# Masking the first key block with a product on VectorE instead of a matmul on TensorE

## The chip, the cores and the metric

The kernel runs on one core of one Trainium2 chip. The metric is the device time of one execution in microseconds (us). The engines are TensorE (PE in the profile; its weight loads are listed apart as PEld), VectorE (DVE), ScalarE (ACT), GpSimd (POOL) and SyncE (SP), which issues most DMAs.

## The reference, cut to what matters

For 32 sequences of 256 tokens with 256 features, a conditioned state-space block is computed first, and its output goes through two layers of windowed attention and feed-forward:

```python
x = x + ffn(cond(x, cond_2048, ...), ...)

# cond: a projection, a causal convolution of 4 taps, a layer norm, then a scan over the tokens
h = clip(h * ad + bd * xt, -10, 10);  yt = ct @ h          # 16 states x 512 channels

# ffn: two layers of
q, k, v = split(shift_token(x) @ wqkv)                     # 8 heads of 64
q, k = rotary(l2norm(q) * qs), rotary(l2norm(k) * ksc)
sim = 8 * q @ k.T                                          # windows of 128 tokens
mask = (i < j) | (i > j + WINDOW) | (j == -1)              # own window and the one before it
x = x + softmax(where(mask, -max, sim)) @ v @ wo
x = x + (a * gelu(g)) @ w2 + b2                            # feed-forward after a layer norm
```

A sequence has two windows of 128 tokens. The first block of keys (keys 0 to 127) is read by all 256 queries: for queries 0 to 127 only keys at or before the query count, for queries 128 to 255 only keys at most 128 tokens back. The second block of keys is read by queries 128 to 255 alone.

## The kernel before

**Groups and units.** The 32 sequences form four groups of 8 (`GB`). Each group first goes through the state-space scan (`group_scan`), 256 steps in 8 chunks of 32, and then through two layers of attention and feed-forward, one sequence at a time. One sequence in one layer is called a unit here; there are 64 units, 16 for each group. The scan of group 0 runs alone at the start; the scans of groups 1, 2 and 3 run beside the units of the group before. In the last group no scan is left.

**Order.** The program writes an order out by hand: a unit has 8 stages (`ST`), and `stage(n, i, what)` puts a piece of work of unit n into stage i. After each stage `scan_to` lets the scan go on by its share of steps. Most of a unit's work overlaps with that of its neighbours: in a stage there may be the projections of the next unit, the scores of this one, and the feed-forward of the two or three before it. Each engine works through its own queue in the order that results, and `keep_in_program_order` pins some instructions there.

**PSUM.** All matmul results go through one pool of 8 banks (`ps_w`), whatever their use. A bank is free again when the engine that reads it is done, so TensorE can have to wait for a reader on another engine before it starts on unrelated work.

**Scores.** The attention computes scores transposed: keys on partitions, queries along the row. Two heads share 128 rows of the transposed queries and keys (64 features each), index r. In stage 2 `scores` works on two parts, and on one more in stage 3; a part is (kw, i0, n), a key block, a first pair of heads and a number of pairs. Key block 0 comes as two parts of two pairs, (0, 0, 2) and (0, 2, 2), and each fills two banks of 2 x 256 columns; key block 1 is one part of four pairs. In the first three groups (`apart` is false) the mask of key block 0 is written into the bank before the scores: a matmul of a bf16 identity with the mask tile `mask_t` (0 or -32768), L1200, and the products are added on top (L1227). These products are cut into four tiles of the array, 64 rows x 64 columns, since a half of 64 keys needs only 192 of the 256 queries. In the last group (`apart` is true) there is no mask matmul; the products run on two row tiles of 64 x 128 over all 256 queries.

**Exponentials and masks.** `exponentials` (L1239, ScalarE) turns the banks into `pT` tiles in SBUF. `mask` then zeroes what is left to mask: for key block 1 by GpSimd's affine select (L1250), and, in the last group, for key block 0 by VectorE's product with `mask_1`, a bf16 tile of zeros and ones (L1255), 128x512 an instruction and four of them a unit, in stages 3 and 4:

```python
masked = nc.vector.tensor_mul(p, p, bc(mask_1[:, 0:nq], 1, n))
```

**Afterwards.** Stage 7 forms the sums (L1264) and the values (L1282) from `pT`. In the next unit the sums make a round trip through DRAM, VectorE divides (L1322), and `project_out` (L1047) multiplies by wo.

**Names of the other lines.** L991: projection of q, k and v. L1007, L1012, L1017 on VectorE and L1015, L1021 on GpSimd: rotary embedding and norms. L1027: scaling by the norm, VectorE. L1036: transposes of q and k. L1402, L1413, L1420: the feed-forward's first product, its gelu on ScalarE, the product of the halves on VectorE. L1429, L1440: its second product and, on VectorE, the residual sum (`narrow`, in stages 3 and 4, ahead of the masks). L1448: the final sum on GpSimd, in the second layer only. Of the scan: L473 to L511 the convolution, shared by GpSimd (L480) and VectorE (L491, L511); L708 scaling a row on ScalarE; L718 a step on VectorE; L730 its read-out on TensorE; L781 and L801 sums and gates of the read-out on VectorE, each freeing a PSUM bank; L787 the transposes between them.

Of the kernel before, what the change touches and what calls it, by code (L numbers as in the profile page):

```python
# [19 lines left out]
P = 128  # L20
S = 256
# [17 lines left out]
W = 128  # L39
# [4 lines left out]
LN_EPS = 1e-5  # L44
CLIP = 10.0
MASKED = -1e30
MASKED_LOW = -32768.0


SCALES2 = 25.0  # L50
# [2 lines left out]
def bc(ap, axis, n):  # L53

    ap = ap.unsqueeze(axis)
    shape = list(ap.shape)
    shape[axis] = n
    return ap.broadcast_to(shape)
# [15 lines left out]
def kernel(  # L74
# [29 lines left out]
    nc = tc.nc  # L104
    B = xT.shape[2]
    L = wqkv.shape[1]
    NG = B // GB

    const = ctx.enter_context(tc.tile_pool(name="const", bufs=1))
# [35 lines left out]
    ident = const.tile([P, P], FP, tag="ident", name="ident")  # L145
# [17 lines left out]
    for j in range(NJ):  # L163
# [12 lines left out]

    mask_t = const.tile([P, 2 * W], BF, tag="mask_t", name="mask_t")
    ident_b = const.tile([P, P], BF, tag="ident_b", name="ident_b")  # L180
    nc.vector.tensor_copy(ident_b, ident)
    nc.gpsimd.memset(mask_t, 0.0)
    nc.gpsimd.affine_select(
        out=mask_t[:, 0:W], in_=mask_t[:, 0:W], compare_op=ALU.is_ge, fill=MASKED_LOW,
        base=0, pattern=[[1, W]], channel_multiplier=-1,
    )
    nc.gpsimd.affine_select(
        out=mask_t[:, W : 2 * W], in_=mask_t[:, W : 2 * W], compare_op=ALU.is_ge,
        fill=MASKED_LOW, base=0, pattern=[[-1, W]], channel_multiplier=1,
    )  # L190

    mask_1 = const.tile([P, 2 * W], BF, tag="mask_1", name="mask_1")
    nc.gpsimd.tensor_scalar(mask_1, mask_t, -1.0, None, ALU.is_ge)

    head_cols = const.tile([P, 2, 32], FP, tag="head_cols", name="head_cols")
    nc.gpsimd.memset(head_cols, 0.0)
# [27 lines left out]
    def program(ctx, exact):  # L224
# [9 lines left out]
        ps_w = ctx.enter_context(tc.tile_pool(name="psw", bufs=8, space=PSUM, reuse_waits="tile"))  # L234
# [822 lines left out]
        if exact:  # L1057
# [104 lines left out]
        class Attention:  # L1162
# [2 lines left out]

            def __init__(self, g, l):
                self.l = l

                self.apart = g == NG - 1
                self.qkv, self.rot, self.p, self.ps, self.o = {}, {}, {}, {}, {}  # L1170

            def project(self, b, w, a):
# [20 lines left out]

            def open_banks(self, kw, n):
                nq = S - kw * W
                banks = []
                for r in range(2):
                    sc = ps_w.tile([P, n, nq], FP, tag="w", name="sc")
                    if kw == 0 and not self.apart:
                        nc.tensor.matmul(  # L1200
                            sc, ident_b, bc(mask_t[:, 0:nq], 1, n), start=True, stop=False
                        )
                    banks.append(sc)
                return banks

            def scores(self, b, *parts):

# [5 lines left out]

            def products(self, b, kw, i0, n, banks):
                qT, kT, _ = self.qkv[b]
                nq = S - kw * W
                masked = kw == 0 and not self.apart
                nm = 2 if masked else 1
                mk = W // nm
                for i in range(n):  # L1220
                    for r in range(2):
                        rows = slice(r * DH, (r + 1) * DH)
                        for m in range(nm):

                            k0 = m * mk
                            q0, q1 = (k0, k0 + W + mk) if masked else (0, nq)
                            nc.tensor.matmul(  # L1227
                                banks[r][k0 : k0 + mk, i, q0:q1],
                                kT[rows, i0 + i, kw * W + k0 : kw * W + k0 + mk],
                                qT[rows, i0 + i, kw * W + q0 : kw * W + q1],  # L1230
                                start=not masked,
                                stop=not masked or i == n - 1,
                            )

            def exponentials(self, b, kw, i0, n, banks):
                nq = S - kw * W
# [245 lines left out]
        def stage(n, i, what, *args):  # L1482
            stages.setdefault(ST * n + i, []).append(partial(what, *args))

        def attend(n, at, b, nxt):

            stage(n, 0, at.turn, b, 1)
            stage(n, 2, at.scores, b, (0, 0, 2), (1, 0, HEADS // 2))
            stage(n, 3, at.scores, b, (0, 2, 2))
            stage(n, 3, at.mask, 1, 0)  # L1490
            if at.apart:
                for i, what in ((3, (0, 0)), (4, (0, 2))):
                    stage(n, i, at.mask, *what)
            stage(n, 7, at.sums, b)
            stage(n, 7, at.values, b)
            stage(n + 1, 0, at.put_sums)
            stage(n + 1, 1, at.load_sums)
            stage(n + 1, 2, at.invert)
            stage(n + 1, 2, at.put_inverse)
            stage(n + 1, 3, at.load_inverse)  # L1500
            stage(n + 1, 5, at.divide, b)
            stage(n + 1, 6, at.finish, b)
            if nxt is not None:
                for w in range(NW):
                    for i, a in ((0, 2), (1, 0), (1, 1)):
# [60 lines left out]
        for t in range(max(stages) + 1):  # L1566
# [3 lines left out]
            g, r = divmod(t + 1 + group - reload, group)  # L1570
# [124 lines left out]
```

## Time and profile before

| | us |
|---|---|
| median of 3 runs | 3545.71 |
| lowest, highest | 3545.69, 3548.17 |
| the profiled execution's own time | 3553.66 |
| its span, first to last instruction | 3551.9 |

| line | what | count | busy us | mean ns of one |
|---|---|---|---|---|
| L1200 | PE, mask product, 128x512 bf16 | 192 | 57.5 | 380 |
| L1227 | PE, products on four tiles, 192 columns | 1536 | 84.6 | 335 |
| L1227 | PE, products on two row tiles, 256 columns | 256 | 36.3 | 402 |
| L1239 | ACT, exponentials | 384 | 202.1 | 603 |
| L1255 | DVE, mask product, 128x512 | 64 | 49.7 | 817 |
| L718 | DVE, scan step | 1024 | 931.9 | 910 |

One execution is profiled, and its times are those of that execution. A float32 matmul that isn't a transpose shows as two records. Matmuls overlap in the array, so the mean length of one is longer than the time from one start to the next; where the cost of a block on TensorE matters, read the time from its first start to the start of what follows. In the order of time, "[0.74 <-DVE zT L801]" says that the engine was idle for 0.74 us before the instruction, and what ended the wait.

### The profile page before, as it was taken

What the parts mean: (1) busy time and instruction counts of PE and PEld (TensorE: products, weight loads), DVE (VectorE), ACT (ScalarE), POOL (GpSimd) and SP (SyncE); (2) the same over time, 40 slices, a digit from 0 to 9 for tenths busy, and PEclk for the clock granted to TensorE, in tenths of its full rate; (3) what the DMA queues carried; (4) which work ended last, traced back from release to release, by engine and by line L of the source; (5) the groups of instructions that cost most, each with busy time, mean ns of one, the idle gap of its engine ahead of it and who ended that gap; (6) DMA issues with size and microseconds to landing.
All of it is one profiled execution on the core that took longest, in us unless ns stands there. A gap on an engine that the chain in (4) does not pass through costs nothing.

```text
span 3551.9 us, 57690 instructions
## 1 busy us (share of the span) xinstructions
PE 3441.7 (97%) x20220; PEld 2263.7 (64%) x20220; DVE 2605.5 (73%) x5049; ACT 2037.4 (57%) x3663; POOL 1620.7 (46%) x1587
## 2 busy tenths in 40 slices
PE   7999989999999999999999999999999999999999
PEld 5445335666666666666666666666666777777777
DVE  4888898877878777877787778787777545555563
ACT  3666656656666656666566656666666444444442
POOL 4433455544545445544454556454443333333441
PEclk8999999999999999999999999999999999999999
DMA  6788765534454555544454445544444212011111
GB/s 183 211 219 217 200 174 153 135 113 134 125 143 138 150 144 150 139 121 126 123 144 131 139 147 146 145 115 129 124 138 118 63 37 62 13 31 35 37 28 38
DMA packets 487199, 436.72 MB, mean 123 GB/s; under 512 B 247155, under 2 KB 326516, under 8 KB 486772
## 3 DMA queue, kind: packets, MB, share of 16 engines
q1 hardware_dynamic: 402450, 420.94, 42.0%
q10 hardware_dynamic: 84450, 12.01, 2.1%
q8 instruction: 162, 2.65, 0.3%
q14 instruction: 137, 1.12, 0.1%
HBM read 384.06 MB, written 47.19 MB: 121 GB/s over the span
## 4 chain that ended last, share of the span: by engine, by line
PE 64%; DVE 16%; DMA 7%; ACT 5%; POOL 4%; issue 3%; SPq 1%; ACTq 0%; DVEq 0%; POOLq 0%
PE ps_qkv L991 13%; PE pa L1402 13%; PE po_f L1429 6%; DVE h L718 6%; DMA xrep<-xnd 5%; PE y L730 5%; PE ps_wo L1047 5%; PE ov L1282 4%; PE ps_in L401 3%; PE ps_out L810 3%; PE sc L1227 3%; PE tr_qk L1036 2%; PE rs L1264 2%; ACT xrep L708 2%; DVE acc L491 2%
## 5 line engine op out<-in xcount | busy, mean ns | idle before, releaser
L718 DVE CUSTOM_DVE_ANT_0 h<-h,xrep,lim 128x512 f32<-128x512 f32 x1024 | 931.9, 910 | 215.1 <-ACT xrep L708 166.5
L708 ACT ACTIVATE xrep<-xrep,beta 128x512 f32<-128x512 f32 x960 | 672.5, 720 | 315.7 <-DMA xrep<-xnd 202.4
L991 PE MATMUL ps_qkv<-qkv,res 128*128 128x512 f32 x1536 | 715.2, 601 | 17.2 <-DVE ag L1420 7.2
L1402 PE MATMUL pa<-hT,w 128*128 128x256 f32 (+1 forms) x2816 | 674.5, 382 | 5.4 <-DVE zT L801 5.1
L1402 PEld LDWEIGHTS pa<-hT,w 128*128 128x128 f32 (+1 forms) x2816 | 517.6, 189 | 145.1 <-issue 38.0
L1015 POOL TENSOR_TENSOR rot<-rot,swp 128x512 f32<-128x512 f32 x256 | 349.0, 1363 | 543.7 <-DVE swp L1012 513.0
L991 PEld LDWEIGHTS ps_qkv<-qkv,res 128*128 128x128 f32 x1536 | 282.2, 191 | 299.8 <-issue 242.2
L1021 POOL TENSOR_TENSOR rn<-ss,neg_half 128x8 f32<-128x8 f32 x256 | 461.0, 1801 | 0.0
L1420 DVE SCALAR_TENSOR_TENSOR ag<-pa,b_sb,ag 128x256 f32<-128x256 f32 x320 | 151.9, 475 | 280.0 <-ACT ag L1413 279.7
L730 PE MATMUL y<-h,ly 128*32 128x512 f32 x2048 | 335.8, 606 | 9.8 <-DVE h L718 9.2
L1429 PE MATMUL po_f<-ag,w 128*128 128x256 f32 x1280 | 305.7, 386 | 1.4 <-DVE fo L1440 0.6
L1354 POOL TENSOR_TENSOR rstd<-ve,neg_half 128x2 f32<-128x2 f32 x64 | 46.1, 720 | 555.9 <-DVE ve L1352 555.9
L1429 PEld LDWEIGHTS po_f<-ag,w 128*128 128x128 f32 x1280 | 235.3, 190 | 64.8 <-DVE xc L511 11.7
L1413 ACT ACTIVATE ag<-pa,b_sb 128x256 f32<-128x256 f32 x320 | 149.9, 469 | 217.8 <-PE pa L1402 215.7
L1004 ACT ACTIVATE sq<-ps_qkv,tiny 128x512 f32<-128x512 f32 x256 | 172.4, 685 | 172.2 <-PE ps_qkv L991 143.8
L1047 PE MATMUL ps_wo<-oT,wo 128*128 128x256 f32 x1024 | 236.2, 385 | 14.2 <-DVE oT L1322 11.2
L1047 PEld LDWEIGHTS ps_wo<-oT,wo 128*128 128x128 f32 x1024 | 196.6, 193 | 45.5 <-issue 9.9
L491 DVE SCALAR_TENSOR_TENSOR acc<-xr,wc_sb,acc 128x256 f32<-128x256 f32 x384 | 188.6, 523 | 46.4 <-POOL acc L480 45.9
L1012 DVE TENSOR_TENSOR swp<-ps_qkv,rs_sb 128x256 f32<-128x256 f32 x512 | 191.8, 416 | 29.8 <-POOL rot L1015 29.6
L1007 DVE TENSOR_TENSOR rot<-ps_qkv,rc_sb 128x512 f32<-128x512 f32 x256 | 173.8, 679 | 45.8 <-ACT sq L1004 45.6
L1239 ACT ACTIVATE pT<-sc 128x512 f32<-128x512 f32 x384 | 202.1, 603 | 7.3 <-PE sc L1227 5.5
L1027 DVE SCALAR_TENSOR_TENSOR rot<-rn,rot 128x512 f32<-128x512 f32 x256 | 196.1, 804 | 5.0 <-POOL rn L1021 4.7
(161 smaller groups left out, 5306.9 us busy)
## 6 DMA issues: line engine op xcount, KB each, us to landing
xrep<-xnd SPq DMA_DIRECT2D x960, 256.0 KB
rb<-inv SPq DMA_DIRECT2D x128, 256.0 KB
xnd<-xn SPq DMA_DIRECT2D x64, 256.0 KB
qkv<-in_wqkv_dram SPq DMA_DIRECT2D x24, 512.0 KB
ahead<-xs_a SPq DMA_DIRECT2D x48, 256.0 KB
xp<-ahead SPq DMA_DIRECT2D x48, 256.0 KB
xd<-xnd SPq DMA_DIRECT2D x192, 64.0 KB
w<-in_w_dram SPq DMA_DIRECT2D x80, 128.0 KB
```

Source lines behind the costliest of these rows:

```text
L491: nc.vector.scalar_tensor_tensor(acc, xr[:, :, k : k + CH], wc_sb[:, ch, k : k + 1], acc, ALU.mult, ALU.add,)
L708: scaled = nc.scalar.activation(bx, ck[c].pop(("bx", t), bx), AF.Copy, scale=ck[c]["beta"][:, t : t + 1])
L718: nc.vector._custom_dve(TENSOR_ADD_SAT, out=h_new, in0=state["h"], in1=bx, s0=ck[c]["lim"][:, 0, t : t + 1], s1=ck[c]["lim"][:, 1, t : t + 1],
L730: nc.tensor.matmul(ck[c]["y", hb][32 * q : 32 * q + 32, :], ly[hb % 2][:, 32 * t : 32 * t + 32], ck[c].pop(("h", hb * TB + t)), start=(i = ...
L991: nc.tensor.matmul(ps, res[b][:, k, t0 : t0 + W], wt["qkv", a][:, k], start=(k == 0), stop=(k == KM - 1),)
L1015: nc.gpsimd.tensor_add(rot, rot, swp)
L1021: nc.gpsimd.tensor_tensor(rn, ss, neg_half, ALU.pow)
L1027: nc.vector.scalar_tensor_tensor(rot, bc(rn, 2, DH), 1e12, rot, ALU.min, ALU.mult)
L1047: nc.tensor.matmul(po[:, d], wt["wo", 0][:, c, d * P : (d + 1) * P], oT[:, c, :], start=(c == 0), stop=(c == NC_ - 1),)
L1239: nc.scalar.activation(p, banks[r], AF.Exp)
L1402: nc.tensor.matmul(dst[x], wt["w1", m][:, k, x], self.h[:, k], start=(k == 0), stop=(k == KM - 1),)
L1429: nc.tensor.matmul(self.po[:, d], wt["w2", 0][:, m, d * P : (d + 1) * P], self.ag[m], start=(m == 0), stop=(m == len(MCH) - 1),)
```

## The change

The way of the last group is used in all four. The mask matmul L1200, `mask_t`, `ident_b` and the flag `apart` go; all products of key block 0 run on two row tiles over all 256 queries; and the four mask products on VectorE a unit are issued in all groups, two in stage 3 and two in stage 4. `mask_1` is built directly by a memset and two affine selects.

```diff
-    mask_t = const.tile([P, 2 * W], BF, tag="mask_t", name="mask_t")
-    ident_b = const.tile([P, P], BF, tag="ident_b", name="ident_b")
-    nc.vector.tensor_copy(ident_b, ident)
-    nc.gpsimd.memset(mask_t, 0.0)
...
     mask_1 = const.tile([P, 2 * W], BF, tag="mask_1", name="mask_1")
-    nc.gpsimd.tensor_scalar(mask_1, mask_t, -1.0, None, ALU.is_ge)
+    nc.gpsimd.memset(mask_1, 1.0)
+    for i, sign in enumerate((1, -1)):
+        half_1 = mask_1[:, i * W : (i + 1) * W]
+        nc.gpsimd.affine_select(
+            out=half_1, in_=half_1, compare_op=ALU.is_ge, fill=0.0,
+            base=0, pattern=[[sign, W]], channel_multiplier=-sign,
+        )
...
-                self.apart = g == NG - 1
...
             def open_banks(self, kw, n):
                 nq = S - kw * W
-                banks = []
-                for r in range(2):
-                    sc = ps_w.tile([P, n, nq], FP, tag="w", name="sc")
-                    if kw == 0 and not self.apart:
-                        nc.tensor.matmul(
-                            sc, ident_b, bc(mask_t[:, 0:nq], 1, n), start=True, stop=False
-                        )
-                    banks.append(sc)
-                return banks
+                return [ps_w.tile([P, n, nq], FP, tag="w", name="sc") for _ in range(2)]
...
                 for i in range(n):
                     for r in range(2):
                         rows = slice(r * DH, (r + 1) * DH)
-                        for m in range(nm):
...
-                            nc.tensor.matmul(
-                                banks[r][k0 : k0 + mk, i, q0:q1],
-                                kT[rows, i0 + i, kw * W + k0 : kw * W + k0 + mk],
-                                qT[rows, i0 + i, kw * W + q0 : kw * W + q1],
-                                start=not masked,
-                                stop=not masked or i == n - 1,
-                            )
+                        nc.tensor.matmul(
+                            banks[r][:, i, :],
+                            kT[rows, i0 + i, kw * W : (kw + 1) * W],
+                            qT[rows, i0 + i, kw * W :],
+                            start=True,
+                            stop=True,
+                        )
...
             stage(n, 3, at.mask, 1, 0)
-            if at.apart:
-                for i, what in ((3, (0, 0)), (4, (0, 2))):
-                    stage(n, i, at.mask, *what)
+            for i, what in ((3, (0, 0)), (4, (0, 2))):
+                stage(n, i, at.mask, *what)
```

More of the change, by code (lines that the diff above doesn't have):

```diff
@@ L46 @@
 MASKED = -1e30
-MASKED_LOW = -32768.0
 SCALES2 = 25.0
@@ L175 @@
     nc.gpsimd.memset(half, 0.5)
-    mask_t = const.tile([P, 2 * W], BF, tag="mask_t", name="mask_t")
-    ident_b = const.tile([P, P], BF, tag="ident_b", name="ident_b")
-    nc.vector.tensor_copy(ident_b, ident)
-    nc.gpsimd.memset(mask_t, 0.0)
-    nc.gpsimd.affine_select(
-        out=mask_t[:, 0:W], in_=mask_t[:, 0:W], compare_op=ALU.is_ge, fill=MASKED_LOW,
-        base=0, pattern=[[1, W]], channel_multiplier=-1,
-    )
-    nc.gpsimd.affine_select(
-        out=mask_t[:, W : 2 * W], in_=mask_t[:, W : 2 * W], compare_op=ALU.is_ge,
-        fill=MASKED_LOW, base=0, pattern=[[-1, W]], channel_multiplier=1,
-    )
-    mask_1 = const.tile([P, 2 * W], BF, tag="mask_1", name="mask_1")
-    nc.gpsimd.tensor_scalar(mask_1, mask_t, -1.0, None, ALU.is_ge)
+    mask_1 = const.tile([P, 2 * W], BF, tag="mask_1", name="mask_1")
+    nc.gpsimd.memset(mask_1, 1.0)
[5 more added lines that the diff above has]
+        )
     head_cols = const.tile([P, 2, 32], FP, tag="head_cols", name="head_cols")
@@ L1195, in open_banks @@
                 nq = S - kw * W
-                banks = []
-                for r in range(2):
-                    sc = ps_w.tile([P, n, nq], FP, tag="w", name="sc")
-                    if kw == 0 and not self.apart:
-                        nc.tensor.matmul(
-                            sc, ident_b, bc(mask_t[:, 0:nq], 1, n), start=True, stop=False
-                        )
-                    banks.append(sc)
-                return banks
+                return [ps_w.tile([P, n, nq], FP, tag="w", name="sc") for _ in range(2)]
             def scores(self, b, *parts):
@@ L1215, in products @@
                 qT, kT, _ = self.qkv[b]
[L1216 to L1219, printed above, removed]
                 for i in range(n):
@@ L1222, in products @@
                         rows = slice(r * DH, (r + 1) * DH)
-                        for m in range(nm):
-                            k0 = m * mk
-                            q0, q1 = (k0, k0 + W + mk) if masked else (0, nq)
-                            nc.tensor.matmul(
-                                banks[r][k0 : k0 + mk, i, q0:q1],
-                                kT[rows, i0 + i, kw * W + k0 : kw * W + k0 + mk],
-                                qT[rows, i0 + i, kw * W + q0 : kw * W + q1],
-                                start=not masked,
-                                stop=not masked or i == n - 1,
-                            )
+                        nc.tensor.matmul(
[5 more added lines that the diff above has]
+                        )
             def exponentials(self, b, kw, i0, n, banks):
```

## The prediction

> **What bounds the kernel now.** I read the page's busy times, then busy time by stretch, then the order of time on TensorE (PE) and VectorE (DVE), then who TensorE waited for. A "unit" below is one sequence in one layer; there are 64, and units 0 to 47 (groups 0 to 2) run from 513 to 2,899 us.
>
> ```profile
> PE 3441.7 (97%) x20220; PEld 2263.7 (64%) x20220; DVE 2605.5 (73%) x5049; ACT 2037.4 (57%) x3663; POOL 1620.7 (46%) x1587
> ```
>
> Busy time by stretch: two neighbouring units of group 1 and one of group 3. Columns are the stretch, its length, then busy time of PE, weight loads, DVE, ACT and POOL, then clock and DMA.
>
> ```profile
> 1432.10:1478.40 46.30, 45.40 (x290) 29.19 (x289) 38.07 (x81) 28.58 (x55) 26.40 (x29) 1.00 0.53 149
> 1478.40:1532.80 54.40, 54.05 (x337) 36.73 (x334) 41.74 (x78) 33.92 (x61) 26.45 (x21) 1.00 0.42 122
> 3131.90:3170.80 38.90, 38.90 (x231) 28.19 (x230) 21.31 (x43) 17.18 (x29) 13.82 (x11) 1.00 0.20 56
> ```
>
> TensorE is full in all three. VectorE is 82% and 77% busy in groups 0 to 2, because the scan of the next group runs beside the attention, and 55% in group 3, where no scan is left. Units come in pairs: a short one (45 to 47 us) that also carries the convolution of a chunk (L474 to L511), and a long one (54 us). Group 3 already runs the code that the change brings to the rest, so its rows price both halves.
>
> **TensorE's saving.** In order of time on TensorE, the two score blocks of a short unit, each with the instruction after it, then those of a unit of group 3 (start, length, line, count):
>
> ```profile
> 1833.03 0.59 PE L1200 MATMUL sc<-mask_t,ident_b 128*128 128x512 bf16 x2
> ...
> 1835.45 2.43 PE L1429 MATMUL po_f<-ag,w 128*128 128x256 f32 x10
> ...
> 1838.59 0.59 PE L1200 MATMUL sc<-mask_t,ident_b 128*128 128x512 bf16 x2
> 1839.11 0.88 PE L1227 MATMUL sc<-qT,kT 64*64 64x192 f32 x16
> 1839.92 1.98 PE L991 MATMUL ps_qkv<-qkv,res 128*128 128x512 f32 x4
> ...
> 3131.91 2.02 PE L1227 MATMUL sc<-qT,kT 64*128 64x256 f32 x24
> 3133.86 2.43 PE L1429 MATMUL po_f<-ag,w 128*128 128x256 f32 x10
> ...
> 3137.09 1.13 PE L1227 MATMUL sc<-qT,kT 64*128 64x256 f32 x8
> 3138.15 1.98 PE L991 MATMUL ps_qkv<-qkv,res 128*128 128x512 f32 x4
> ```
>
> Start to start, the first block takes 1835.45 - 1833.03 = 2.42 us now and 1.95 us in the new form; the second 1839.92 - 1838.59 = 1.33 us and 1.06 us. Two mask products cost 0.52 us a block (1839.11 - 1838.59), 1.04 us a unit; the products on two row tiles give 0.30 us of it back. That leaves 0.74 us a unit, and 48 units make 35.5 us. The memset and selects ahead of everything swap one for one, off the path: nothing.
>
> **VectorE's cost.** Four products of 128x512 a unit, in two pairs A and B, each behind an L1440 of the same stage. In group 3 the pair at 3137.16 is followed by L1027 at 3138.36: a pair holds VectorE for 1.20 us. That is 2.40 us a unit, 115 us in all, on an engine that has 8 to 13 us idle in a unit. The total fits; what counts is where TensorE waits for VectorE. The order of time on VectorE in the short unit, and the waits of TensorE there and in its neighbours ([idle before <- releaser]):
>
> ```profile
> 1839.69 0.81 DVE L718 CUSTOM_DVE_ANT_0 h<-h,xrep,lim 128x512 f32<-128x512 f32 x1 [2.35 <-ACT xrep L708]
> 1840.42 0.48 DVE L1440 SCALAR_TENSOR_TENSOR res<-po_f,b_sb,res 128x256 f32<-128x256 f32 x1
> ...
> 1849.12 0.48 DVE L1440 SCALAR_TENSOR_TENSOR res<-po_f,b_sb,res 128x256 f32<-128x256 f32 x1
> 1849.99 2.75 DVE L491 SCALAR_TENSOR_TENSOR acc<-xr,wc_sb,acc 128x256 f32<-128x256 f32 x6 [0.39 <-POOL acc L480]
> ...
> 1859.64 0.68 DVE L801 TENSOR_TENSOR zT<-tz,sg 128x512 f32<-128x512 f32 x1
> ```
>
> ```profile
> 1460.57 1.78 PE L1402 MATMUL pa<-hT,w 128*128 128x256 f32 x7 [0.74 <-DVE zT L801]
> 1885.65 1.99 PE L991 MATMUL ps_qkv<-qkv,res 128*128 128x512 f32 x4 [0.34 <-DVE xd L781]
> ```
>
> *Short units.* After the wait that ends at 1839.69, VectorE has only four pauses until L801: 0.46, 0.30, 0.39 and 0.27 us, each for GpSimd, and GpSimd is itself waiting for VectorE there. L801 ends at 1860.32 and the L1402 that needs its bank starts at 1860.55: 0.23 us to spare. At 1460.57 in another such unit there is nothing to spare: TensorE stands 0.74 us until L801 is done. The divide L1322 is as tight: it ends at 1854.94, and L1047 starts at 1856.22, 1.28 us later. So everything that pair A and pair B add ahead of L801 reaches TensorE. Pair A, at 1840.8, adds 1.20 us. Behind it on VectorE stand L1027, the convolution, the scan steps and, later, L1322 and L801. Pair B, at 1849.5, covers the pause of 0.39 us (in other units also one of 0.30): it adds 0.51 to 0.81 us. Neither pair waits for its exponentials: those of A end 1.8 us before it, those of B 7 us. VectorE is then 1.7 to 2.0 us late at L801. The wait at 1839.69 does not move forward with the faster scores, because ScalarE reaches the exponentials from a queue that is full from 1832.4 on. Less 0.06 to 0.23 us of room, TensorE comes out about 1.7 us later than now, and the 0.74 us that it won becomes part of a longer wait. From L801 on the two engines are late together, so nothing is added afterwards.
>
> *Long units.* Score block B ends at 1885.3, and L991 then waits for a bank until L781 is done, whose VectorE chain began before the scores. The 0.74 us is lost in that wait. The pairs come after it and then fall into a pause of 4.19 us that TensorE sets (L1420, at 1899.61). I take 0.
>
> *Sum.* Units 14 to 39 are 13 such pairs: 13 x 1.7 = +22 us. Units 0 to 13 are irregular. The bounds are 14 x (-0.74) = -10 and 14 x 1.7 = +24 us. Some wait for L1322 as above and others have pauses of over 1 us in VectorE, so I take 0. Units 40 to 47 have no tight wait (TensorE is busy for 364.00 of the 364 us from 2,500 on): 8 x (-0.74) = -6 us. Group 3 doesn't change. Together +16 us. The profiled execution's own time of 3,553.7 us becomes 3,569.7; the runs' median lies 8.0 us under that execution, which gives 3,562 us.
>
> *A price that is not settled* is a mask beside GpSimd. One pair of group 3, at 2987.74, took 2.35 us where others take 1.28, beside GpSimd's L1448; the pair at 3137.16 ran at full speed beside L1021. L1448 comes only in half of the units, so the bound is 24 x 1.07 = 26 us; I take 0, since in the short unit at 1432 L1448 starts only 1.6 us after the L1440 ahead of pair B. The Trainium skill's page "SBUF — State Buffer", section "SBUF: two separate sides", speaks against the change here: a VectorE operation with two SBUF inputs and a GpSimd operation that reads SBUF exclude each other for a whole instruction. By that rule every mask that meets GpSimd would wait; the row at 2987.74 agrees, the row at 3137.16 does not, and by the rule the sum would be nearer +42 than +16 us.
>
> **Rivals.**
> 1. *TensorE keeps its saving* (faster). The waits on L801, L781 and L1322 are for banks or for work laid out with some room; banks are dealt out anew, and VectorE's lag could then be taken up by other banks. For it: TensorE's waits for these three lines sum to only 22 us of the 3,552 us span (table of waits: 11.2 for L1322, 6.8 for L801, 4.5 for L781), and group 3 carries the same masks with no wait. Against: group 3 has no scan, and L801 leaves TensorE 0.2 us at most. It gives 3,545.7 - 35.5 = 3,510; with half of it lost, 3,528.
> 2. *The lag costs more.* Nothing is covered (2.40 us in each of about 23 units that carry a convolution, +55), L1448 meets half of them (+12), less 6: +61, 3,607 us.
> 3. *It cancels.* The irregular units gain 10 us and the short ones lose only 1 us: within 7 us of 3,546.
> 4. *The change doesn't do what it says*, so that a mask comes ahead of its exponentials in VectorE's queue and holds it. In group 3 no idle time stands before any of the 64 masks; I fold this into the second.
>
> **How the numbers follow.** About 0.2% (7 us) is what a measurement here can tell from no change. Forecast (+8 to +35 us) 0.50, rival 2 0.20, rival 1 0.20, rival 3 0.10. That is faster 0.20, same 0.10, slower 0.70. The range of the forecast alone is 3,554 to 3,581. The 8 in 10 range reaches into both rivals: 3,520 to 3,604, and leaves out about half of each, 2 in 10.
>
> **What would show it.** Right: L1200 gone; L1227 at 1.95 and 1.06 us a unit everywhere; 256 masks at L1255 with about 0.60 us each; short units of about 47 to 48 us, with TensorE's waits for L801 and L1322 grown from single tenths to 1 or 2 us each; long units still 54 us. Wrong: long units of 53.6 us and short ones of 45 us, with TensorE's waits no larger (rival 1), or masks of over 1 us (rival 2).

## The result and the profile after

The changed kernel took 3,554.9 us (median of 7 runs, 3,552.85 to 3,563.63), the kernel before 3,545.71 (median of 7, 3,541.25 to 3,548.17). The ratio is 1.0031, with a 95% interval of 1.0019 to 1.0042: slower by 0.3%. The profiled execution of the changed kernel took 3,554.36 us with a span of 3,552.6, that of before 3,553.66. The profile of before thus lies 8 us above its median and that of after at its own, so the two spans, added up, hide the loss. Stretches from the middle of the program can still be compared one by one. Lines moved: those of the scan, the projections and the rotary embedding by 8 (L801 is now L793, L781 is L773, L718 is L710, L491 is L483, L730 is L722, L991 is L983, L1012 is L1004), those from the scores on by 26 (L1227 is L1201, L1255 is L1229, L1322 is L1296, L1402 is L1376, L1420 is L1394, L1448 is L1422).

The busy line of the page after:

```profile
PE 3421.0 (96%) x19260; PEld 2262.9 (64%) x19260; DVE 2725.2 (77%) x5240; ACT 2030.6 (57%) x3663; POOL 1622.9 (46%) x1586
```

VectorE got 119.8 us busier (2,605.5 before), against 115 predicted; TensorE lost only 20.7 us of busy time. Busy time by stretch (columns as in the prediction): the same short unit as there, and the long one behind it.

```profile
1439.30:1485.50 46.20, 45.19 (x271) 29.56 (x272) 39.91 (x85) 28.56 (x55) 26.61 (x29) 1.00 0.55 149
1485.50:1540.00 54.50, 53.56 (x314) 36.84 (x314) 43.80 (x83) 33.82 (x63) 26.42 (x21) 1.00 0.43 126
```

The short unit has 1.84 us more of VectorE (38.07 before) and is no longer than before (46.30); the long one has 0.49 us less of TensorE (54.05 before) and is no shorter (54.40). The order of time on TensorE says why, first the short unit, then the score block and what follows in the long one:

```profile
1439.33 2.02 PE L1201 MATMUL sc<-qT,kT 64*128 64x256 f32 x24
1441.29 2.42 PE L1403 MATMUL po_f<-ag,w 128*128 128x256 f32 x10
...
1444.51 1.13 PE L1201 MATMUL sc<-qT,kT 64*128 64x256 f32 x8
1445.57 1.99 PE L983 MATMUL ps_qkv<-qkv,res 128*128 128x512 f32 x4
...
1467.37 1.99 PE L1376 MATMUL pa<-hT,w 128*128 128x256 f32 x8 [0.74 <-DVE zT L793]
...
1490.74 1.14 PE L1201 MATMUL sc<-qT,kT 64*128 64x256 f32 x8 [0.26 <-DVE swp L1004]
1492.55 1.98 PE L983 MATMUL ps_qkv<-qkv,res 128*128 128x512 f32 x4 [0.68 <-DVE xd L773]
```

The blocks take 1.96 and 1.06 us, start to start, as forecast. The wait for L793 is 0.74 us, just what it was before in this unit (1460.57 there): the short unit did not get its extra 1.7 us. In the long unit the wait for the bank of L773 grew from 0.35 us (before, in this unit) to 0.68, and one of 0.26 for L1004 stands before the scores: the saving is lost there, about half of it in the forecast wait.

By stage, from the profiles (a unit starts with its first score block; us):

| units | before | after | difference | predicted |
|---|---|---|---|---|
| 0 to 3 | 180.3 | 190.7 | +10.4 | 0 to 13 together: 0 |
| 4 to 13 | 535.9 | 535.7 | -0.2 | |
| 14 to 39 | 1307.7 | 1308.2 | +0.5 | +22 |
| 40 to 47 | 361.4 | 356.7 | -4.7 | -6 |

Each stretch is that of one execution. Only4 below shows how far such a stretch scatters: where its program is that of before, its units 4 to 13 are 2.7 us shorter and its units 14 to 39 3.8 us longer.

The loss stands at the beginning. Busy time of units 0 to 3 in four kernels: before, the changed one, and two of the experiments (the change from unit 14 on; the change in units 0 to 3 alone).

```profile
513.40:693.70 180.30, 169.73 (x1068) 100.64 (x1067) 158.83 (x303) 116.94 (x215) 106.17 (x102) 0.98 0.50 139
```

```profile
508.20:698.90 190.70, 173.71 (x989) 102.38 (x988) 171.66 (x327) 118.14 (x216) 106.83 (x103) 0.97 0.47 133
```

```profile
511.30:690.90 179.60, 169.71 (x1067) 101.16 (x1065) 158.04 (x303) 117.28 (x215) 107.33 (x102) 0.97 0.50 139
```

```profile
509.30:700.30 191.00, 174.13 (x987) 102.58 (x986) 169.99 (x324) 117.97 (x216) 106.73 (x102) 0.97 0.48 132
```

VectorE is busy for 88% of this stretch before (158.83 of 180.30), against 79% in units 14 to 39 (1,032.11 of 1,307.7). Where the masks are here, VectorE has 11 to 13 us more to do (16 masks at 0.60 us are 9.6 of it, and five to eight other instructions fell into the stretch), and the stretch is 10 to 11 us longer. The granted clock (the third number from the end) does not separate them: 0.97 without the masks in the third row, at 179.60 us, and with them in the second. What grew most is TensorE's wait for the scan steps, in these units before and after (us in total, times, longest):

```profile
PE y L730 <- DVE h L718: 2.0, 2, 1.2
```

```profile
PE y L722 <- DVE h L710: 6.9, 6, 1.8
```

The wait for the divide grew from 2.1 to 4.2 us there.

### The profile page after: what moved, and what is told of

It reads as the page before. It is cut to its first block, busy times and chain, and to the rows that moved or that the text cites. A ratio compares the mean times of both kernels' runs of the same rounds, so it can differ in the third digit from the quotient of the medians.

```text
span 3552.6 us, 55958 instructions
## 1 busy us (share of the span) xinstructions
PE 3421.0 (96%) x19260; PEld 2262.9 (64%) x19260; DVE 2725.2 (77%) x5240; ACT 2030.6 (57%) x3663; POOL 1622.9 (46%) x1586
## 4 chain that ended last, share of the span: by engine, by line
PE 62%; DVE 18%; DMA 7%; ACT 5%; POOL 5%; issue 3%; SPq 0%; ACTq 0%; POOLq 0%; DVEq 0%
PE ps_qkv L983 13%; PE pa L1376 13%; DVE h L710 7%; PE po_f L1403 6%; PE ps_wo L1039 5%; DMA xrep<-xnd 4%; PE y L722 4%; PE ov L1256 4%; PE ps_out L802 3%; PE sc L1201 3%; PE ps_in L393 3%; PE tr_qk L1028 2%; PE rs L1238 2%; DVE acc L483 2%; ACT xrep L700 2%
## 5 line engine op out<-in xcount | busy, mean ns | idle before, releaser
L710 DVE CUSTOM_DVE_ANT_0 h<-h,xrep,lim 128x512 f32<-128x512 f32 x1024 | 932.3, 910 | 135.5 <-ACT xrep L700 101.3
L983 PE MATMUL ps_qkv<-qkv,res 128*128 128x512 f32 x1536 | 716.9, 602 | 22.4 <-DVE ag L1394 9.4
L1376 PE MATMUL pa<-hT,w 128*128 128x256 f32 (+1 forms) x2816 | 674.3, 382 | 4.4 <-DVE zT L793 4.4
L1376 PEld LDWEIGHTS pa<-hT,w 128*128 128x128 f32 (+1 forms) x2816 | 516.9, 188 | 144.4 <-issue 41.7
L1007 POOL TENSOR_TENSOR rot<-rot,swp 128x512 f32<-128x512 f32 x256 | 350.3, 1368 | 536.5 <-DVE swp L1004 517.6
L983 PEld LDWEIGHTS ps_qkv<-qkv,res 128*128 128x128 f32 x1536 | 282.5, 191 | 308.5 <-issue 249.1
L1013 POOL TENSOR_TENSOR rn<-ss,neg_half 128x8 f32<-128x8 f32 x256 | 460.5, 1799 | 0.0
L722 PE MATMUL y<-h,ly 128*32 128x512 f32 x2048 | 346.9, 606 | 16.2 <-DVE h L710 13.8
L1394 DVE SCALAR_TENSOR_TENSOR ag<-pa,b_sb,ag 128x256 f32<-128x256 f32 x320 | 152.0, 475 | 229.1 <-ACT ag L1387 228.4
L1039 PE MATMUL ps_wo<-oT,wo 128*128 128x256 f32 x1024 | 240.0, 389 | 18.6 <-DVE oT L1296 15.9
L483 DVE SCALAR_TENSOR_TENSOR acc<-xr,wc_sb,acc 128x256 f32<-128x256 f32 x384 | 186.5, 510 | 51.1 <-POOL acc L472 50.9
L1004 DVE TENSOR_TENSOR swp<-ps_qkv,rs_sb 128x256 f32<-128x256 f32 x512 | 192.0, 416 | 30.8 <-POOL rot L1007 30.6
L1201 PE MATMUL sc<-qT,kT 64*128 64x128 f32 (+1 forms) x2048 | 202.9, 337 | 3.4 <-DVE swp L1004 2.6
```

The lines of the kernel that those rows point to most:

```text
L483: nc.vector.scalar_tensor_tensor(acc, xr[:, :, k : k + CH], wc_sb[:, ch, k : k + 1], acc, ALU.mult, ALU.add,)
L710: nc.vector._custom_dve(TENSOR_ADD_SAT, out=h_new, in0=state["h"], in1=bx, s0=ck[c]["lim"][:, 0, t : t + 1], s1=ck[c]["lim"][:, 1, t : t + 1],
L722: nc.tensor.matmul(ck[c]["y", hb][32 * q : 32 * q + 32, :], ly[hb % 2][:, 32 * t : 32 * t + 32], ck[c].pop(("h", hb * TB + t)), start=(i = ...
L983: nc.tensor.matmul(ps, res[b][:, k, t0 : t0 + W], wt["qkv", a][:, k], start=(k == 0), stop=(k == KM - 1),)
L1007: nc.gpsimd.tensor_add(rot, rot, swp)
L1013: nc.gpsimd.tensor_tensor(rn, ss, neg_half, ALU.pow)
```

## The experiments

Four kernels at a time shared their runs of the kernel before: 3,543.4 us in the first four, 3,543.8 in the second, 3,554.9 in the third. So ratios, not times, compare kernels of different fours. One bound on the reading of profiles: the stretch ahead of unit 0, whose code is nearly the same in all but after_x18, took from 501.7 to 514.0 us (522.9 in after_x18).

| label | time | ratio to before | 95% interval | units 0-3 | 4-13 | 14-39 | 40-47 |
|---|---|---|---|---|---|---|---|
| t_half | 3540.9 | 0.9993 | 0.9984 to 1.0002 | 183.2 | 529.2 | 1306.9 | 356.6 |
| v_half | 3598.3 | 1.0155 | 1.0141 to 1.0169 | 190.0 | 546.1 | 1348.3 | 361.4 |
| from14 | 3537.2 | 0.9983 | 0.9974 to 0.9992 | 179.6 | 534.9 | 1305.8 | 356.6 |
| after_x18 | 3569.8 | 1.0073 | 1.0060 to 1.0087 | 187.7 | 538.2 | 1309.1 | 356.8 |
| v_half_d4 | 3558.5 | 1.0041 | 1.0027 to 1.0056 | 188.8 | 537.1 | 1312.6 | 362.0 |
| before_d4 | 3550.4 | 1.0018 | 1.0006 to 1.0029 | 177.5 | 527.8 | 1320.6 | 361.4 |
| after_d4 | 3559.1 | 1.0035 | 1.0021 to 1.0049 | 187.7 | 542.6 | 1311.4 | 358.8 |
| from14_d4 | 3534.4 | 0.9974 | 0.9965 to 0.9983 | 177.8 | 531.2 | 1308.9 | 358.4 |
| only4 | 3561.1 | 1.0021 | 1.0007 to 1.0035 | 191.0 | 533.2 | 1311.5 | 361.4 |
| from4 | 3556.7 | 1.0004 | 0.9990 to 1.0018 | 182.2 | 540.4 | 1310.1 | 356.7 |
| twice | 3619.4 | 1.0186 | 1.0170 to 1.0202 | 197.6 | 549.8 | 1347.6 | 359.4 |
| best | 3539.6 | 0.9960 | 0.9946 to 0.9974 | 180.7 | 534.4 | 1305.2 | 356.7 |

### The two halves apart: t_half and v_half

TensorE's half alone, with the masks of key block 0 left out in groups 0 to 2: the changed kernel with

```diff
+                self.apart = g == NG - 1
...
-            for i, what in ((3, (0, 0)), (4, (0, 2))):
-                stage(n, i, at.mask, *what)
+            if at.apart:
+                for i, what in ((3, (0, 0)), (4, (0, 2))):
+                    stage(n, i, at.mask, *what)
```

> TensorE's half alone: no mask matmul, two row tiles, and no mask at all on key block 0 in groups 0 to 2 (that part of the computation is left out). If TensorE's own work sets the pace everywhere, 48 units save 0.74 us each: 35 us less than before, about 3,510 us. If TensorE stands at VectorE's results in the paired units 14 to 39, as the prediction had it, only units 0 to 13 and 40 to 47 save: 22 x 0.74 = 16 us, about 3,530 us, and the long units stay at 54 us with a longer wait for the bank of xd.

Measured: 0.9993 of before, 2.5 us, an interval that holds no change, and less than either of the two sums expected (16 and 35 us). TensorE's busy time fell by 28 us (3,441.7 to 3,413.8) and hardly any of it reaches the end. Units 14 to 39, before and in t_half:

```profile
1229.60:2537.30 1307.70, 1290.84 (x8061) 856.86 (x8060) 1032.11 (x2042) 813.72 (x1483) 670.98 (x629) 1.00 0.49 136
```

```profile
1222.60:2529.50 1306.90, 1276.97 (x7543) 861.80 (x7542) 1033.73 (x2042) 813.09 (x1483) 650.01 (x629) 1.00 0.49 136
```

TensorE's busy time fell by 13.9 us and the stretch by 0.8; the rest became waits. In units 40 to 47, where TensorE waits for nothing, 4.8 us came through. TensorE, 97% busy, does not set the pace of units 14 to 39 in the sense that a microsecond taken from it is won. (Of units 4 to 13 this can't be said: they are 6.7 us shorter in this one profile.)

VectorE's half alone: the kernel before with

```diff
-            if at.apart:
-                for i, what in ((3, (0, 0)), (4, (0, 2))):
-                    stage(n, i, at.mask, *what)
+            for i, what in ((3, (0, 0)), (4, (0, 2))):
+                stage(n, i, at.mask, *what)
```

> VectorE's half alone: the kernel before, with its mask matmuls, plus the four mask products a unit on VectorE in all groups (the second mask changes no value). If VectorE's queue keeps its order (the prediction), every short unit grows by 1.7 us and the irregular units by as much: 45 us over before, about 3,590 us. If the program's builder moves unpinned work (convolution taps) behind the late results, the pairs cost almost nothing and the irregular units some 10 to 25 us: 3,555 to 3,570 us, and fewer than 12 taps stand ahead of zT in a short unit.

Measured: 1.0155, 55 us slower, and units 14 to 39 took 40 of them. The number is near the first of the two expected, but not for its reason: fewer than 12 taps stand ahead of zT, the sign of the second. The halves give -2.5 and +55 us, and together +11: they do not add up, so something else differs between these kernels. It is, for the larger part, the order on VectorE, as the next section shows. The program pins only some instructions; the others are laid out by what is ready, and that is worked out anew for every kernel. The order on VectorE in the short units from 16 to 38, as the programs have it (h a scan step, X L781, M a mask, r L1027, c a convolution tap L491, D the divide L1322, "rww." a rotary block L1007 and L1012 with L1017, Z L801, a dot anything else):

```
before     hXh.h..h.rr..cccccc..h..h...cccccc...Drww.rww.hZ
after      hXh.h..h.MMrr..cccch..hcc.MM....c.Drww.rww.hZ
v_half     hXh.h..h.MMrr..ccccch..h..MMc..cc.rww.rww.DhZ
v_half_d4  hXh.h..h.MMrr..ccccch..h..DMMc...rww.rww.hZ
twice      h.M.MM.Mrrch..hcc.McMM.Mc.rww.rww.DhZ
```

Before, all 12 taps of the chunk stand ahead of Z. After, 7 do; the other five went to the pause behind Z. In the short unit at 1439 they are here, in the order of time on VectorE:

```profile
1446.93 1.28 DVE L1229 TENSOR_TENSOR pT<-pT,mask 128x512 f32<-128x512 f32 x2
...
1455.50 1.28 DVE L1229 TENSOR_TENSOR pT<-pT,mask 128x512 f32<-128x512 f32 x2
...
1459.87 0.49 DVE L483 SCALAR_TENSOR_TENSOR acc<-xr,wc_sb,acc 128x256 f32<-128x256 f32 x1 [1.74 <-POOL acc L472]
...
1460.68 1.24 DVE L1296 TENSOR_TENSOR oT<-oT,rb 128x1024 f32<-128x1024 f32 x1
...
1466.63 0.69 DVE L793 TENSOR_TENSOR zT<-tz,sg 128x512 f32<-128x512 f32 x1
...
1476.71 1.66 DVE L483 SCALAR_TENSOR_TENSOR acc<-xr,wc_sb,acc 128x256 f32<-128x256 f32 x4
```

Four taps take 1.66 us, so five are worth about 2.1 us: nearly the 2.4 us of the two mask pairs that came in ahead of L793. That arithmetic fits the unchanged wait of 0.74 us, but it wasn't isolated: no version with all taps ahead of L793 and nothing else moved was run.

### The place of the divide: v_half_d4, before_d4, after_d4

In v_half and in twice the divide stands behind both rotary blocks. One edit moves it, in three kernels:

```diff
-            stage(n + 1, 5, at.divide, b)
+            stage(n + 1, 4, at.divide, b)
```

> The masks alone, as in v_half, with one thing changed: the divide (L1322 there) is traced one stage earlier (stage 4 of the next unit instead of 5). In v_half's queue on VectorE the builder put the next unit's two rotary blocks (L1007, L1012, L1017, 11 operations with L1027's followers, about 4 us) ahead of the divide in every short unit from 14 on, and TensorE waited 15 times for L1322, 51.1 us in all; with the earlier stage the divide stands ahead of mask pair B and of the rotary blocks. Theory (the place of the divide made v_half dear, not the 115 us of masks): the 51 us of waits for L1322 fall under 10 us, units 14 to 39 come back from 1348 to about 1315 us, units 0 to 13 from 736 to 722 or less, the time from 3598 to about 3555. Rival A (VectorE's load made it dear): the lag shows up at the next hand-over, L801, with waits of about 40 us; the time stays within 10 us of 3598. Rival B (half and half): about 3575.

Measured: 3,558.5 us, 40 us less than v_half with the same masks and the same arithmetic. The table of TensorE's waits, of v_half and then of v_half_d4 (us in total, times, longest):

```profile
PE ps_wo L1047 <- DVE oT L1322: 51.1, 15, 5.0
PE y L730 <- DVE h L718: 15.1, 18, 3.4
```

```profile
PE y L730 <- DVE h L718: 18.4, 20, 3.6
...
PE sc L1200 <- DVE swp L1012: 9.9, 14, 1.0
...
PE ps_qkv L991 <- DVE xd L781: 7.2, 15, 0.5
```

The 51.1 us for the divide are gone from the list, and units 14 to 39 came back from 1,348.3 to 1,312.6 us. The theory holds and rival A falls: not the load made v_half dear, but one instruction behind about 4 us of others in its queue, with TensorE waiting for it. (The edit also let other unpinned instructions move; the two queues are shown above. And units 0 to 13 came back to 725.9 us only, not to 722 or less.) By the ratios the halves now add up: 0.0041 less t_half's 0.0007 makes 0.0034, and the whole change with the divide at this place, after_d4 below, has 0.0035.

Waiting is little more than half of what the late divide cost. Units 14 to 39 of v_half and of v_half_d4:

```profile
1242.30:2590.70 1348.40, 1306.17 (x8062) 869.63 (x8061) 1121.30 (x2146) 821.14 (x1483) 652.07 (x629) 0.98 0.47 132
```

```profile
1229.70:2542.40 1312.70, 1290.64 (x8062) 856.63 (x8061) 1092.70 (x2146) 811.92 (x1484) 675.16 (x629) 1.00 0.48 135
```

Of the 35.7 us between them 15.5 are TensorE's busy time, with the same 8,062 instructions, and the granted clock is 0.98 against 1.00. One of the waits in v_half:

```profile
1370.60 6.62 PE L1047 MATMUL ps_wo<-oT,wo 128*128 128x256 f32 x16 [3.58 <-DVE oT L1322]
```

These 16 matmuls take 6.45 us from their first start to the next instruction's at 1377.05, against 3.45 before (1856.22 to 1859.67), and the granted clock from 1369.8 to 1376.4 is 0.50. Nine of the twelve waits for L1322 in this stretch, of 2.6 to 5.0 us, have such a spell of 3.4 or 6.8 us at half the clock that begins during the wait.

> The kernel before with the divide (L1322) traced one stage earlier; no other edit. It gives the price of that stage without the change, so that after_d4 minus before_d4 is the change with the divide out of the way. Here five convolution taps stand between the divide and the rotary blocks in a short unit, 12 taps still ahead of L801. Theory (the divide's waits are real but in few units): the 11.2 us of waits for L1322 in units 0 to 13 go, the time is 3535 to 3540, and after_d4 lies 0 to 8 us above it. Rival A: others take over, 3543 to 3548. Rival B (the change's cost is not the divide's): after_d4 stays 9 us or more above before_d4.

Measured: 1.0018, 6.6 us slower than before, a miss of theory and rival A; rival B, which asked for 9 us between after_d4 and this kernel, is missed by a little (8.8 between the medians). Units 0 to 13 gained 11 us in the profile, and units 14 to 39 lost 13: there the divide now has five taps between it and the rotary blocks (short units 47.1 us on average, 46.1 before).

> The changed kernel with the divide (L1296) traced one stage earlier; nothing else. In the changed kernel TensorE waited for L1296 five times, 15.9 us (before 11.2 us in four). Theory (most of the +10 us in units 0 to 13 is the divide coming late behind the masks): those waits fall under 4 us, units 0 to 13 go from 726 to about 715 us, the time from 3555 to about 3543; short units from 14 on unchanged within 0.3 us each. Rival A (VectorE is simply late, whatever comes first): L793 and L773 take over the waits, the time stays 3550 to 3560. Rival B (the divide, now earlier, waits for its inverse from memory and holds VectorE): over 3565.

Measured: 1.0035, as the changed kernel (1.0031). TensorE's waits for L1296, 15.9 us in five before the edit, are gone, but the scores' wait for L1004 rose from 2.6 to 10.1 us, the steps' wait (L722 for L710) from 13.8 to 18.4 and L773's from 7.2 to 10.2: rival A. With the divide out of the way in both, the change costs 3,559.14 - 3,550.36 = 8.8 us between the medians and 6 by the ratios, against 9.2 and 11 without: within the intervals, of some 5 us each, the same. So late divides are not shown to be what makes the change a loss.

### Where the loss stands: from14, only4, from4

> The change applied from unit 14 on; units 0 to 13 keep the mask matmul. If the loss sits in the irregular units 0 to 13 (+10 us there in the profiles), it is gone: 3,539 to 3,545 us, level with before or just under it. If the loss sits in the paired units as predicted, it stays: about 3,560 us.

The edit, in the kernel before, with n the number of the unit and `apart` now an argument (the mask products are issued where it is true):

```diff
-                self.apart = g == NG - 1
+                self.apart = apart
...
-        ats = [Attention(g, l) for g, l, _ in seqs]
+        ats = [Attention(g, l, n >= 14) for n, (g, l, _) in enumerate(seqs)]
```

Measured: 0.9983, 6.2 us faster than before. The same change is a gain from unit 14 on, 4.8 us of it in units 40 to 47, and a loss ahead of it. This kernel and the changed one differ in units 0 to 13 alone, and by 0.0048 of the time, about 17 us.

> The change in units 0 to 3 alone (four units of 48); all others keep the mask product on TensorE. In the profiles, units 0 to 3 take 180.3 us before, 179.6 in from14, but 190.7 with the change and 188 to 190 in every kernel that has the masks on VectorE there, whatever the place of the divide; VectorE is busy there for 158.8 of 180.3 us before (88%, against 79% in units 14 to 39). Theory (VectorE sets the pace of these four units, and its 9.6 us of masks come out in full): units 0 to 3 take 188 to 191 us, all others as before within 2 us, the time 3551 to 3555, so four units bring the whole loss of the changed kernel. Rival A (the loss is spread over all 14 irregular units): 3545 to 3549. Rival B (the profiles' differences there are the noise of one execution): 3541 to 3547.

The edit: `n < 4 or g == NG - 1` in place of `n >= 14`. Measured: 1.0021, 7.5 us at that kernel's time, 2.5 to 12.4 by the interval. Four units of 48 bring 7.5 us, where the whole change, with the gain of its later units in it, loses 11 by its ratio. In the profile units 0 to 3 take 191.0 us, as predicted. The order on VectorE does not decide here as it does in the short units: the six kernels with these masks, in several orders, took 187.7 to 191.0 us for units 0 to 3, and the seven without took 177.5 to 183.2. Counted from the launch, so that work shifted across the boundary doesn't matter, unit 4 starts at 700.3 us, in the changed kernel at 698.9, in v_half at 696.2; in the kernels with the same place of the divide but no such masks there (before, t_half, from14, from4) at 690.9 to 693.7. With the earlier divide it starts at 692.7 (v_half_d4) and 696.9 (after_d4) with the masks, and at 679.5 (from14_d4) and 680.8 (before_d4) without; best, at 691.3, is an exception, and its unit 0 starts 7 to 9 us later than in these two.

> The complement of only4: the change in units 4 to 47, the mask product kept on TensorE in units 0 to 3. Theory (the loss is in units 0 to 3): within 3 us of from14, 3535 to 3541, although ten more units carry the masks. Rival A (spread over units 0 to 13): 3544 to 3548, some 8 us above from14. Rival B (noise): 3550 to 3556, as the changed kernel.

The edit: `n >= 4` in place of `n >= 14`. Measured: 1.0004, 7 us above from14 where rival A asked for 8 and the theory for 3 at most: rival A's number. Units 0 to 3 are near before (182.2 us). From14 and from4 differ by ten units, 4 to 13, and by 0.0021 of the time, about 7 us, with intervals that just overlap; their profiles put 5.5 us there (534.9 and 540.4), while the changed kernel, with the same masks, took 535.7. With only4 it adds up: 7.5 and 1.4 us make 8.9, near the 9 to 11 of the whole change. Over all profiles of the table, units 4 to 13 took 535.7 to 546.1 us in the six kernels that have single masks there and 527.8 to 535.9 in the seven that have none. So units 0 to 3 are shown to cost; that units 4 to 13 together cost about as much is likely, and its size is not settled.

### Dose: twice

The changed kernel, with `twice` true in groups 0 to 2:

```diff
+                        if not kw and self.twice:
+                            tc.keep_in_program_order(
+                                nc.vector.tensor_mul(p, p, bc(mask_1[:, 0:nq], 1, n))
+                            )
```

> The changed kernel with every mask of units 0 to 47 applied twice (the factors are 0 and 1, so the product is the same): 4.8 us of VectorE a unit instead of 2.4. The builder's order for it has the divide behind the two rotary blocks again in every short unit from 14 on, as in v_half. Theory (the order decides, load counts where VectorE sets the pace): units 0 to 3 about 10 us longer again (200), short units 50 to 53 us as in v_half, so units 14 to 39 near 1350 to 1370 us, the time 3605 to 3640. Rival A (VectorE has room in units 14 to 39 and takes them as it took the first): units 14 to 39 within 10 us of 1308, the time 3565 to 3575. Rival B (every microsecond of mask reaches the end from here on): 3555 + 115 = 3670.

Measured: 1.0186, in the theory's span at before's earlier time (3,611.7 on 3,545.7); rivals A and B fall. Units 0 to 3 took 6.9 us longer again (197.6; about 10 was expected), and units 14 to 39 1,347.6 us, with TensorE's waits for the divide up from five to 19, 57.0 us in all. That is v_half's figure with twice its masks: in units 14 to 39 the first 2.4 us a unit cost 0.5 us in all, and the same masks in another order, or double masks in that order, 40 us. The dose alone was not separated from the order here.

### The long units: after_x18

```diff
-                    at(s + 21, gated, c, hb)
+                    at(s + 18, gated, c, hb)
```

> The change, with the sum into xd (gated) traced three steps of the scan earlier, which puts it one scan step (0.72 us) sooner in VectorE's queue. If TensorE's saving in the long units is lost in the wait for the bank that this sum frees, each of some 13 long units gets 0.7 us shorter: about 9 us under the change, 3,546 us. If something else holds the long units at 54 us, nothing moves: 3,555 us.

Measured: 1.0073, a miss. Long units take 54.7 us (54.3 in the changed kernel), so the saving wasn't freed; part of the wait of 0.68 us now stands before the scores, for the same L773. The edit also reaches the scan of group 0, which runs alone: unit 0 starts at 522.9 us instead of 508.2, a difference of 14.7 us, as large as the whole 15 (other kernels reach 514.0 there, so not all of it need be the edit's). The experiment says nothing on what long units would gain by an earlier L773 alone.

### What the runs point to: from14_d4 and best

> The change from unit 14 on only (units 0 to 13 keep the mask product on TensorE), with the divide traced one stage earlier in all units. from14 alone took 3537. Theory (late divides are what is left of TensorE's waits in units 0 to 13, about 11 us, and they add up with the change's gain of about 5 us after unit 40): 3527 to 3533. Rival A: another producer takes over the waits: 3537 within 4 us. Rival B (the divide holds VectorE): over 3545.

The edit: from14 with the stage of the divide as in v_half_d4. Measured: 0.9974, faster than both kernels, by its time in rival A's span and 1.4 us above the theory's. Units 0 to 13 took 709.0 us (from14 714.5), half of the gain that the theory had; units 14 to 39 took 1,308.9 us where from14 had 1,305.8, so here the earlier divide cost a little from unit 14 on.

> What the runs point to: the change from unit 14 on only, the divide traced one stage earlier for units 0 to 13 only. In the profiles the earlier divide brought units 0 to 13 from 716 to 705 to 709 us and cost 3 to 13 us from unit 14 on. Theory (the two add up): 3526 to 3532, faster than both kernels. Rival A (the gain of the earlier divide was one execution's): 3535 to 3539 as from14. Rival B (the seam between the two stages costs a wait at unit 14): over 3540.

The edit, in from14: `stage(n + 1, 4 if n < 14 else 5, at.divide, b)`. Measured: 0.9960, 0.9946 to 0.9974, that is 14 us under the kernel before (3,531.5 on its 3,545.7, within the theory's span; the raw 3,539.6 stands beside 3,554.9 for before). It beats both kernels. Its advantage over from14_d4 is within the intervals, and its profile does not show where it comes from: units 0 to 13 take 715.1 us there, as in from14 (714.5). The theory's number came out here, its reason did not show.

## Why the prediction was right, and where not

**The sign was right and the size nearly, and the size by luck: two terms of the sum were wrong and offset each other.** Forecast +16 us, measured +9 to +11. By the runs, units 0 to 13 cost about 15 us (only4's 7.5 and the 7 between from4 and from14) where the sum had 0, and units 14 to 47 gain 6 (from14) where it had a loss of 16.

*TensorE's saving, 0.74 us a unit*: right in the blocks (1.96 and 1.06 us). That it is lost in units 14 to 39 and comes through behind them was right too: t_half won 0.8 us in units 14 to 39 and 4.8 in units 40 to 47. Rival 1, which let TensorE keep 17 to 35 us, falls by this run alone, before any mask is added.

*VectorE's cost, 1.20 us a pair*: right, 1.20 us at 1446.93 (to the L1019 at 1448.13) and 119.8 us of busy time.

*Short units, +22 us*: wrong. The failing step is "everything that pair A and pair B add ahead of L801 reaches TensorE", with the list of what stands behind the masks taken over from the trace of before. The queue was not that list with two pairs put in. Five taps left the tight stretch, and short units went from 46.1 to 46.0 us, not to 47 or 48. The sign that was named for being right, waits for L801 and L1322 of 1 or 2 us each in these units, did not come: TensorE's waits for L793 ahead of L1376 sum to 4.4 us in six over the whole program, after 5.1 in seven before. The lag itself is no fiction: with the queue of v_half it costs 40 us there and 55 in total, near rival 2's +61, by waits for L1322, the line that the prediction named as just as tight, and by the lower clock that goes with them, which the prediction did not have. What decided between +22, +40 and +0.5 was a layout that the trace of before can't show.

*Long units, 0*: right, 54.3 us after 54.4, about half by the named wait (0.33 of the 0.74 us in the unit shown) and 0.26 by one just before it.

*Units 0 to 13, 0*: mis-sized. The bounds of -10 to +24 us held, the chosen middle did not: +10.2 us in the profile, about 15 by the runs. The prediction looked at single waits in these units and took the mean of two sorts. The rows by stretch would have separated units 0 to 3: VectorE is 88% busy there, and 16 masks of 0.60 us are 9.6 us on an engine with little room. Only4 gives 7.5 us for them.

*Units 40 to 47, -6*: -4.7, right.

*The mask beside GpSimd*: the price was in L1448 as suspected, but in the short units GpSimd paid it, not VectorE. The order of time on VectorE and on GpSimd around one mask pair of a late unit, and on GpSimd in the short unit above:

```profile
2697.01 2.36 DVE L1229 TENSOR_TENSOR pT<-pT,mask 128x512 f32<-128x512 f32 x2
...
2697.18 1.64 POOL L1422 TENSOR_TENSOR fo<-fo,xs 128x512 f32<-128x512 f32 x1 [4.29 <-DVE fo L1414]
```

```profile
1455.67 3.58 POOL L1422 TENSOR_TENSOR fo<-fo,xs 128x512 f32<-128x512 f32 x1
...
1459.28 0.56 POOL L472 TENSOR_SCALAR acc<-xr,wc_sb,bconv_sb 128x256 f32<-128x256 f32 x1
```

At 2697 the pair took 2.36 instead of 1.28 us: the second mask, at 2697.61, takes 1.76 us and ends 0.55 us after L1422 does. At 1455 the masks ran at full speed, L1422 took 3.58 us (1.26 before, at 1449.80), and the taps waited 1.74 us for the L472 behind it. The masks are not the only ones that held it: L503 and L466, with two inputs as well, follow them without a pause until 1458.13, and L1422 ends 1.12 us after that. Nor was the meeting new: before, beside L1448 at 1449.80, five taps took 3.06 us where five take 2.07 at 1443.10, so there VectorE paid. The Trainium skill's page "SBUF — State Buffer", section "SBUF: two separate sides", calls this an exclusive lock that goes to whoever starts first, for a whole instruction; these rows agree with a lock held for whole instructions. In the prediction the sum by that rule was +42 us; the measured loss is about a quarter of it.

## What to carry to other kernels

Take an engine's share of busy time stage by stage before pricing added work: at 88%, in units 0 to 3, the masks came out nearly in full; at 79%, in units 14 to 39, they cost between nothing and 40 us, decided by what stood ahead of the one instruction that TensorE waits for. Such a wait can cost twice: after 3.58 us of it the next 16 matmuls took 6.45 us instead of 3.45, at half the clock. Where a builder lays out unpinned work, an added instruction moves others; price the change with the queue of the changed program, not with the old one. And a change that loses in one stage and gains in another can be taken in the second alone: from unit 14 on it is 0.2% faster than before.

## What the runs showed of the hardware

VectorE's mask (two SBUF inputs) and GpSimd's instructions on 128x512 tiles hold each other up, in both directions. Of the 256 masks, 78 that met no GpSimd instruction in groups 0 to 2 took 0.68 us at the median; beside L1422 (GpSimd, two inputs) a mask took 0.68 or 1.76 us and nothing between; beside L1224 (GpSimd's affine select, one tensor) mostly 0.73 or 1.11 us, with a median of 1.11 over 37 masks. Beside L1013 and L559, GpSimd's small powers, the mask stayed at 0.68. Which of two waiting instructions goes first was not settled: the second mask waited for L1422 at 2697 and overtook it at 1455, with the same 0.17 us between the first mask's start and L1422's.
